# Three edits in the recurrence of a four-layer graph kernel: earlier masks on GpSimd, and a DRAM round trip issued by ScalarE

## The chip, the cores and the metric

The kernel runs on one core of one Trainium2 chip. The metric is the device time of one execution in microseconds, lower being better. Engines are named as in the profile: PE (TensorE, with PEld for its weight loads), DVE (VectorE), ACT (ScalarE), POOL (GpSimd) and SP (SyncE, which here only issues DMAs and waits).

## The reference

Four layers over x and adj, both of shape 64 x 256 x 256 in float32; each layer is followed by a residual and a layer norm. Only layer 0 is touched. It is a gated recurrence over the 256 nodes of each of the 64 graphs:

```python
d = jnp.sum(adj, axis=-1)
dinv = jnp.where(d != 0, 1.0 / jnp.where(d != 0, d, 1.0), 0.0)
norm_adjT = jnp.swapaxes(adj, 1, 2) * dinv[:, :, None]

def step(h, i):
    x = jnp.take(h_e, i, axis=1)
    row = jnp.take(norm_adjT, i, axis=1)
    x_par = jnp.einsum('bj,bjd->bd', row, h)
    iou = x @ W_ioux.T + b_ioux + x_par @ W_iouh.T + b_iouh
    r, z = jnp.split(iou, 2, axis=1)
    r, z = (jax.nn.sigmoid(r), jax.nn.sigmoid(z))
    hc = jnp.tanh(x @ W_coux.T + b_coux + x_par * r @ W_couh.T + b_couh)
    h_new = z * x_par + (1.0 - z) * hc
    h = jax.lax.dynamic_update_slice(h, h_new[:, None, :], (0, i, 0))
    return (h, None)
h_out, _ = jax.lax.scan(step, h_e, jnp.arange(n))
```

h starts as x itself, so the parent sum x_par of node i takes the new states of nodes j < i and the inputs x of nodes j >= i, weighted by adj[j, i] / d[i]. Layers 1 to 3 (a graph convolution and two attentions) follow graph by graph.

## The kernel before

The step over the nodes is serial, and all 64 graphs go through it together: a tile holds 128 partitions, two halves of the 256 features times 64 graphs. One step is a chain: the parent sum xp is transposed on PE (L610), copied by ACT (xpT, L612), multiplied with the weights on PE (L603), put through a sigmoid by ACT (L826), multiplied by xp on DVE (L828), transposed and copied again (rT), multiplied, put through tanh by ACT (L860), and combined on DVE to the next xp (L862, L865). The xp of the next step also takes v (DVE L851), which needs `ready` (POOL L802), the sum gathered so far for that node.

The sums of a block of U = 8 nodes lie in a tile ACC. They are gathered from several sides:

- The x side (nodes j >= i, whose state is still x). For the first 128 nodes it is done ahead of the recurrence. For the others `x_side` does it in 16 groups of 4 graphs beside steps 0 to 79: a tile xA (adj, 128 x 4 x 128) and a tile xX (x) are loaded on SP, xA is multiplied by the triangle `tri` on POOL (`cut`, L332), matmuls follow on PE (L212), and the product goes to DRAM (Us). `x_side` is a generator that the steps with p = n mod 8 of 4 to 7 advance, when no matmul of the early side is at hand.
- The early side: whole earlier blocks of states, read back from DRAM (Hs, with A from adj), multiplied on PE (L416) and sent through DRAM (Es).
- The late side (`late`): states of the last blocks, kept in a ring Hw in SBUF, against a table An, which is adj's tile `raw` masked by a window on POOL (`late_load`, L477). There is one table for each 32 nodes. Its matmuls (PE L519) run in steps p = 0 to 3; ACT copies the products to lb (L255); `send` writes lb to DRAM as Lb in two DMAs (L499), `receive` reads it back as late_sb one step later (L505), and POOL adds it to ACC after the steps p = 5 and 6 (L874).
- The nearest states, added on DVE (L628) and POOL (L661, L665).

The order on each engine is written out by hand: the instructions stand on each engine in the order in which the Python emits them, and each engine works through its own in order. `at_step(n, f)` emits f at the end of step n, after the step's own instructions. Loads of the x side, the early side and the tables go through a list sorted by rank (`load_later`), of which two are issued in each step with p < 4 (`next_load`); `landed` is a guess that is true from three steps after the issue. `cut` of `late_load` first issues what is left of its four loads. All these DMAs are on SP's queue, and so are sends, receives and the DMAs that put each new state hs into the ring (L654). In the built program a DMA takes one of eight completion semaphores, and before it is issued its engine waits until the DMA that used that semaphore last has landed.

Of the kernel before, what the change touches and what calls it, by code (L numbers as in the profile page):

```python
# [70 lines left out]
def _recurrence(tc, ident, Hd, x, adj, W_ioux, b_ioux, W_iouh, b_iouh, W_coux, b_coux, W_couh, b_couh, wide, then):  # L71
# [19 lines left out]
    nc = tc.nc  # L91
    B, N, D = x.shape
# [6 lines left out]
    XB = 4  # L99
    NG = B // 4  # L100
    HB = B // 2
    FAR = (2, 4, 4, 4, 4, 4, 3, 4)

    with ExitStack() as ctx:
# [84 lines left out]
        for w in range(2):  # L189
            first = (w * T - W + T // 2) % W  # L190
# [18 lines left out]
        def x_product(pb, at, A, Xs):  # L209

            for jc, (a, xs) in enumerate(zip(A, Xs)):
                nc.tensor.matmul(  # L212
                    pb[:, at, :], a, xs, start=(jc == 0), stop=(jc == len(A) - 1)
                )

        def x_out(half, b, ub):

            for c in range(2):
                nc.sync.dma_start(
                    Us[c, b:b + 4, half * P:(half + 1) * P, :].rearrange("b i f -> i b f"),  # L220
                    ub[:, :, c * P:(c + 1) * P],
                )
# [26 lines left out]
        def next_load(n):  # L249
            if loads:  # L250
                loads.pop(0)[1](n)

        def copy_later(out, in_, then=None):
            def f(n):
                nc.scalar.copy(out, in_)  # L255
                held.pop(0)
                if then:
                    then(n)

            copies.append(f)  # L260

        def load_later(out, in_, rank):

            begun = []

            def f(n):
                with nc.allow_non_contiguous_dma(reason="bias vector across partitions"):
                    nc.sync.dma_start(out, in_)
                begun.append(n)

            loads.append((rank, f))
            loads.sort(key=lambda e: e[0])
            return begun

        def landed(begun, n):

            return all(f and n > f[0] + 2 for f in begun)

        def at_step(n, f):
            transfers.setdefault(n, []).append(f)  # L280
# [3 lines left out]
        def base_bank(shape, name):  # L284

            while len(held) == 3:
                next_of(copies, now)
            held.append(name)
            return ps.tile(shape, F32, tag="base", name=name, bufs=3)
# [29 lines left out]
        ahead = []  # L319

        def x_side():

            def load(g):
                A = stream.tile([P, XB, P], F32, tag="xA", name=f"xA2_{g}", bufs=3)
                Xs = stream.tile([P, XB, D], F32, tag="xX", name=f"xX2_{g}", bufs=3)
                return A, Xs, [
                    load_later(to, of.rearrange("b j d -> j b d"), 2)
                    for to, of in ((A, adj[g:g + XB, P:N, P:N]), (Xs, x[g:g + XB, P:N, :]))
                ]

            def cut(A):
                nc.gpsimd.tensor_mul(A, A, tri.unsqueeze(1).to_broadcast([P, XB, P]))  # L332

            tiles = [load(e * XB) for e in range(3)]
            ahead = False
            n = yield
            for g in range(0, B, XB):
                A, Xs, last = tiles.pop(0)
                while not ahead:
                    if landed(last, n):  # L340
                        cut(A)
                        ahead = True
                    n = yield
                ub = stream.tile([P, 4, D], F32, tag="ub", name=f"xu2_{g}")
                for b in range(0, XB, 2):
                    pb = base_bank([P, 2, D], f"xp2_{g}_{b}")
                    for q in range(2):
                        x_product(pb, q, [A[:, b + q, :]], [Xs[:, b + q, :]])
                        if q:
                            copy_later(ub[:, b:b + 2, :], pb, None if b + 2 < XB else (  # L350
                                lambda n, b=g, ub=ub: at_step(n + 1, lambda: x_out(1, b, ub))
                            ))
                            if b + 2 == XB:
                                ahead = bool(tiles) and landed(tiles[0][2], n)
                                if ahead:
                                    cut(tiles[0][0])
                                if g + 3 * XB < B:
                                    tiles.append(load(g + 3 * XB))
                        n = yield


# [90 lines left out]
        def late_load(k, n=None):  # L452


            An = blk.tile([P, HB, U, T // U], F32, tag="An", name=f"An_{k}")
            raw = stream.tile([P, HB, T], F32, tag="raw", name=f"raw_{k}", bufs=1)
            first, last = k * T - W + T // 2, k * T + T // 2
            if first < 0:
                nc.gpsimd.memset(raw, 0.0)
            begun = []  # L460
            for lo, hi, at in ring(max(first, 0), last):
                for g in range(2):
                    to = raw[g * W + at:g * W + at + hi - lo]
                    of = adj[g * HB:(g + 1) * HB, lo:hi, k * T:(k + 1) * T].rearrange(
                        "b j i -> j b i"
                    )
                    if n is None:
                        nc.scalar.dma_start(to, of)
                    else:
                        begun.append(load_later(to, of, 1.5))  # L470

            def cut(lo):
                while not all(begun):
                    next_load(now)
                part = raw[:, lo:lo + HB // 4].rearrange("p b (s u) -> p b s u", u=U)
                take = window[k % 2].rearrange("p (s u) -> p s u", u=U).unsqueeze(1)
                nc.gpsimd.tensor_mul(  # L477
                    An[:, lo:lo + HB // 4].rearrange("p b u s -> p b s u"), part,
                    take.to_broadcast(list(part.shape)),
                )  # L480

            for e in range(4):
                if n is None:
                    cut(e * HB // 4)
                else:
                    at_step(n + 20 + e, lambda e=e: cut(e * HB // 4))
            return An

        def late(first):

            k, i = divmod(first, T)
            An = tables[k]["An"]
            lb = stream.tile([P, NG, D], F32, tag="lb", name=f"lb_{first}", bufs=1)
            Lb = dram.tile([2, NG, 4, U, P], F32, tag="Lb", name=f"Lb_{first}")
            sides[first] = blk.tile([P, U, P], F32, tag="late", name=f"late_sb_{first}", bufs=1)

            def send():
                for c in range(2):
                    nc.sync.dma_start(  # L499
                        Lb[c].rearrange("n q u f -> (q u) n f"),  # L500
                        lb[i // U::T // U, :, c * P:(c + 1) * P],
                    )

            def receive():
                nc.sync.dma_start(sides[first], Lb.rearrange("c n q u f -> (c n q) u f"))  # L505

            def then(n):
                at_step(n, send)
                at_step(n + 1, receive)

            n = yield
            for u in range(0, NG // 2, 2):
                pb = [base_bank([P, 2, D], f"late_{first}_{u}_{g}") for g in range(2)]
                for e in range(2):
                    for q in range(4):
                        for g in range(2):
                            rows = slice(g * W, (g + 1) * W)
                            b = (u + e) * 4 + q
                            nc.tensor.matmul(  # L519
                                pb[g][q * T:(q + 1) * T, e, :],  # L520
                                An[rows, b].rearrange("p u s -> p (u s)"),
                                Hw[rows, b, :], start=True, stop=True,
                            )
                    if e:
                        for g in range(2):
                            at = g * NG // 2 + u
                            copy_later(
                                lb[:, at:at + 2, :], pb[g],
                                then if g and u + 2 == NG // 2 else None,
                            )  # L530
                    n = yield
# [137 lines left out]
        sides = {}  # L669
# [8 lines left out]
        with tc.tile_pool(name="r_first_ps", bufs=4, space=bass.MemoryType.PSUM) as xps:  # L678
            for g in range(0, B, GB):
# [4 lines left out]
                for n in range(0, GB, 4):  # L684
                    ub = fst.tile([P, 4, D], F32, tag="ub", name=f"xu_{g}_{n}")
                    for e in range(0, 4, 2):
                        pb = xps.tile([P, 2, D], F32, tag="x", name=f"xp_{g}_{n}_{e}")
                        for q in range(2):
                            b = n + e + q
# [66 lines left out]
        for now in range(N):  # L756
            n = now
# [30 lines left out]
            r, c = rc[:, 0, :], rc[:, 1, :]  # L788
# [685 lines left out]
```

## Time and profile before

| | |
|---|---|
| Median of 3 runs | 3467.49 us (3466.55 to 3467.74) |
| The profiled execution's own time | 3469.95 us |
| Its span, first to last instruction | 3468.2 us |
| Mean granted TensorE clock | 0.976 |
| Recurrence, read from the trace | about 139 to 1560 us |
| Layers 1 to 3 | about 1560 to 3468 us |

How to read it: busy time is counted for each engine, without the instructions that only wait or issue DMAs. A line of the waits reads "engine tile line <- what ended the wait: us in total, times, longest". A line of the timeline reads start, duration, engine, source line, operation, tile written <- tiles read, and in brackets the idle time of the engine just before it with what ended it. A q after an engine's name is its queue of DMA issues.

### The profile page before, as it was taken

What the parts mean: (1) busy time and instruction counts of PE and PEld (TensorE: products, weight loads), DVE (VectorE), ACT (ScalarE), POOL (GpSimd) and SP (SyncE); (2) the same over time, 40 slices, a digit from 0 to 9 for tenths busy, and PEclk for the clock granted to TensorE, in tenths of its full rate; (3) what the DMA queues carried; (4) which work ended last, traced back from release to release, by engine and by line L of the source; (5) the groups of instructions that cost most, each with busy time, mean ns of one, the idle gap of its engine ahead of it and who ended that gap; (6) DMA issues with size and microseconds to landing.
All of it is one profiled execution on the core that took longest, in us unless ns stands there. A gap on an engine that the chain in (4) does not pass through costs nothing.

```text
span 3468.2 us, 80349 instructions
## 1 busy us (share of the span) xinstructions
PE 3243.9 (94%) x29350; PEld 2331.3 (67%) x29350; DVE 2505.5 (72%) x7061; ACT 1883.5 (54%) x5010; POOL 1874.3 (54%) x2165
## 2 busy tenths in 40 slices
PE   5699999899899898887999999999999999999997
PEld 4555555555555555555888888888888888888885
DVE  3376766766666777754888888887888887888885
ACT  0254545545444454444666666666666666666664
POOL 2366676766566777743444444444444444444443
PEclk8999999999999999997999999999999999999999
DMA  9755576687787575321111111111111111111100
GB/s 293 228 156 138 159 178 153 154 187 194 188 207 166 143 174 146 97 58 58 47 46 47 47 47 46 47 47 46 47 46 46 47 47 46 47 47 46 47 29 21
DMA packets 389348, 347.89 MB, mean 100 GB/s; under 512 B 107356, under 2 KB 355304, under 8 KB 383720
## 3 DMA queue, kind: packets, MB, share of 16 engines
q1 hardware_dynamic: 371256, 325.82, 35.0%
q10 hardware_dynamic: 17696, 16.91, 1.5%
q8 instruction: 235, 3.85, 0.5%
q14 instruction: 161, 1.32, 0.1%
HBM read 224.01 MB, written 99.61 MB: 93 GB/s over the span
## 4 chain that ended last, share of the span: by engine, by line
PE 73%; DVE 7%; DMA 7%; POOL 5%; issue 4%; ACT 3%; SPq 2%; ACTq 0%; DVEq 0%; POOLq 0%
PE mm L995 13%; PE rc L603 5%; PE s L1179 4%; PE rc L595 4%; PE mm_2f L995 3%; PE mm_3v L995 3%; PE mm_t L995 3%; PE late L519 3%; PE mm_3f L995 3%; PE mm_2v L995 3%; PE mm_g L995 3%; PE mm_2s L995 3%; DVE ACC L628 3%; PE o L1214 3%; PE mm_2w L995 3%
## 5 line engine op out<-in xcount | busy, mean ns | idle before, releaser
L628 DVE SCALAR_TENSOR_TENSOR ACC<-keep,S,ACC 128x128 f32<-128x128 f32 x1712 | 504.3, 345 | 189.9 <-ACT hs L646 172.4
L1191 POOL TENSOR_TENSOR p3s<-p 128x256 f32<-128x256 f32 x512 | 387.6, 788 | 366.5 <-ACT p L1189 366.0
L995 PE MATMUL mm<-xT,weights 128*128 128x256 f32 x2048 | 481.9, 383 | 2.9 <-ACT xT L1077 2.9
L995 PEld LDWEIGHTS mm<-xT,weights 128*128 128x128 f32 x2048 | 384.8, 190 | 79.4 <-issue 25.5
L1188 DVE TENSOR_TENSOR p<-s,neg 128x512 f32<-128x512 f32 x512 | 317.7, 683 | 114.3 <-PE s L1179 114.3
L665 POOL TENSOR_TENSOR ACC<-ACC,far 128x384 f32<-128x384 f32 (+1 forms) x313 | 372.6, 1190 | 24.5
L595 PE MATMUL rc<-WxT,xqT 128*64 128x256 f32 x2048 | 330.2, 401 | 4.2 <-ACT rc L836 1.2
L661 POOL TENSOR_TENSOR far<-hs,S 128x384 f32<-128x384 f32 (+1 forms) x313 | 304.9, 974 | 4.7
L802 POOL TENSOR_TENSOR ready<-ACC,dinv 128x128 f32<-128x128 f32 x255 | 102.3, 401 | 369.6 <-DVE ACC L628 369.4
L959 ACT ACTIVATE y<-y,shift,rstd 128x256 f32<-128x256 f32 x512 | 273.4, 599 | 48.0 <-DVE shift L957 43.8
L1189 ACT ACTIVATE p<-p 128x512 f32<-128x512 f32 x512 | 295.0, 627 | 2.1 <-DVE p L1188 1.6
L1102 ACT ACTIVATE qk<-mm,weights 128x256 f32<-128x256 f32 x256 | 107.5, 471 | 268.9 <-PE mm L995 268.9
L1091 POOL TENSOR_TENSOR y<-y,g 128x512 f32<-128x512 f32 x64 | 81.1, 1267 | 267.5 <-issue 267.5
L1228 DVE RECIPROCAL rT<-o 128x256 f32<-128x256 f32 x128 | 223.8, 1748 | 0.3 <-PE o L1205 0.2
L947 DVE BATCH_NORM_STATS2 st<-y 128x6 f32<-128x256 f32 x512 | 209.0, 408 | 13.4 <-POOL y L1091 12.7
L951 POOL TENSOR_TENSOR rstd<-rstd,mhalf 128x2 f32<-128x2 f32 x256 | 173.8, 697 | 82.5 <-DVE rstd L950 80.7
L612 ACT COPY xpT<-xpT_ps 128x128 f32<-128x128 f32 x256 | 68.4, 267 | 259.7 <-PE xpT_ps L610 259.7
L603 PE MATMUL rc<-WhT,xpT 128*64 128x128 f32 x2048 | 171.3, 289 | 29.1 <-ACT xpT L612 28.6
L1056 POOL TENSOR_TENSOR dis<-dis,mhalf 128x2 f32<-128x2 f32 x64 | 44.9, 702 | 277.3 <-DVE dis L1055 260.7
L603 PEld LDWEIGHTS rc<-WhT,xpT 128*64 128x64 f32 x2048 | 108.4, 138 | 119.9 <-ACT xpT L612 84.2
L212 PE MATMUL xp<-xX,xA 128*128 128x256 f32 x384 | 115.7, 446 | 59.3 <-POOL xA L681 32.6
L1154 ACT ACTIVATE qk<-mm,weights 128x256 f32<-128x256 f32 x256 | 107.5, 471 | 115.9 <-PE mm L995 115.9
(162 smaller groups left out, 7501.7 us busy)
## 6 DMA issues: line engine op xcount, KB each, us to landing
xX<-in_x_dram ACTq DMA_DIRECT2D x16, 1024.0 KB
Us<-xu SPq DMA_DIRECT2D x64, 256.0 KB
xq<-in_x_dram SPq DMA_DIRECT2D x64, 256.0 KB
ACC<-Us SPq DMA_DIRECT2D x32, 512.0 KB
Es<-eu SPq DMA_DIRECT2D x64, 256.0 KB
early_sb<-Es SPq DMA_DIRECT2D x32, 512.0 KB
xin<-in_x_dram SPq DMA_DIRECT2D x64, 256.0 KB
ad<-in_adj_dram SPq DMA_DIRECT2D x64, 256.0 KB
```

The source lines that it names most:

```text
L595: nc.tensor.matmul(G[o * B:(o + 1) * B], xqT[a, i // 2][:, i % 2, kc, h * B:(h + 1) * B], WxT[:, kc, o, gates], start=False, stop=False, s ...
L603: nc.tensor.matmul(G[o * B:(o + 1) * B], hT[:, kc * B:(kc + 1) * B], WhT[:, kc, o, g], start=False, stop=(kc == 1), skip_group_check=True,)
L628: nc.vector.scalar_tensor_tensor(acc[:, 0, :], keep[:, j % 2, :], s, acc[:, 0, :], ALU.mult, ALU.add)
L661: nc.gpsimd.tensor_mul(tmp[:, 0:count, :], hs.unsqueeze(1).to_broadcast(shape), s.unsqueeze(2).to_broadcast(shape),)
L665: nc.gpsimd.tensor_add(acc, acc, tmp[:, 0:count, :])
L947: nc.vector.bn_stats(st, y[:, c, :])
L959: nc.scalar.activation(y[:, c, :], y[:, c, :], AF.Identity, bias=shift[:, c:c + 1], scale=rstd[:, c:c + 1],)
L995: nc.tensor.matmul(pm[:, c, :], lhsT[:, k, c * P:(c + 1) * P], rhs[:, k, :], start=(k == 0), stop=(k == 1),)
L1188: nc.vector.tensor_add(p, s_ps[i], self.neg3)
L1189: nc.scalar.activation(p, p, AF.Exp, scale=ISQ)
L1191: nc.gpsimd.tensor_add(both, p[:, 0, :], p[:, 1, :])
L1228: nc.vector.reciprocal(rT, o_ps[:, 1, :])
```

## The change

Three edits, all in layer 0:

1. `x_side` looks for the next group's tile at each of its turns and masks it as soon as its loads count as landed, instead of only at the last matmul of the group before it.
2. The four masks of a late table are emitted at the ends of steps 12, 15, 20 and 23 of the 32 before the table is needed, instead of 20, 21, 22, 23.
3. `send` and `receive` of the late side are issued by ACT instead of SP.

```diff
@@ x_side
                     n = yield
+                ahead = False
                 ub = stream.tile([P, 4, D], F32, tag="ub", name=f"xu2_{g}")
...
-                            if b + 2 == XB:
-                                ahead = bool(tiles) and landed(tiles[0][2], n)
-                                if ahead:
-                                    cut(tiles[0][0])
-                                if g + 3 * XB < B:
-                                    tiles.append(load(g + 3 * XB))
+                            if b + 2 == XB and g + 3 * XB < B:
+                                tiles.append(load(g + 3 * XB))
+                        if not ahead and tiles and landed(tiles[0][2], n):
+
+                            cut(tiles[0][0])
+                            ahead = True
                         n = yield
@@ late_load
-                    at_step(n + 20 + e, lambda e=e: cut(e * HB // 4))
+                    at_step(n + (12, 15, 20, 23)[e], lambda e=e: cut(e * HB // 4))
@@ late
             def send():
                 for c in range(2):
-                    nc.sync.dma_start(
+                    nc.scalar.dma_start(
                         Lb[c].rearrange("n q u f -> (q u) n f"),
                         lb[i // U::T // U, :, c * P:(c + 1) * P],
                     )
 
             def receive():
-                nc.sync.dma_start(sides[first], Lb.rearrange("c n q u f -> (c n q) u f"))
+                nc.scalar.dma_start(sides[first], Lb.rearrange("c n q u f -> (c n q) u f"))
```

## The prediction

> **What bounds the kernel now.** I first read the busy time by stages (stretches 0 to 139, 139 to 1560, 1560 to 3468 us). The 256 recurrence steps, layer 0, are the middle one, and all three edits lie in it. The last stage, with PE busy for 1868.80 of 1908.20 us, has none of their instructions.
>
> ```profile
> 0.00:139.00 139.00, 82.16 (x308) 64.00 (x308) 39.63 (x61) 2.83 (x4) 28.35 (x21) 0.82 0.95 286
> 139.00:1560.00 1421.00, 1292.94 (x16498) 766.57 (x16493) 976.55 (x3348) 700.31 (x2445) 964.09 (x1056) 0.98 0.63 156
> 1560.00:3468.20 1908.20, 1868.80 (x12550) 1500.72 (x12550) 1489.34 (x3653) 1180.33 (x2561) 881.91 (x1088) 0.99 0.14 45
> ```
>
> (Busy us of PE, PEld, DVE, ACT, POOL; PE's clock; DMA share; GB/s.) No engine is full here: a step is a chain PE transpose, ACT copy, PE, ACT sigmoid, DVE, PE, ACT tanh, DVE. I took each step's length from the timeline, as the distance between starts of the xpT transposes (PE L610). With p = n mod 8, the medians for p = 0 to 7 are 5.31, 5.16, 5.16, 5.47, 5.51, 5.14, 4.96, 5.46 us, so anything over about 6 is a stall. Their waits over the stretch:
>
> ```profile
> POOL ACC L874 <- DMA late_sb<-Lb: 40.0, 10, 7.5
> DVE keep L851 <- POOL ready L802: 25.3, 9, 5.4
> PEld xp L212 <- POOL xA L332: 16.5, 7, 3.0
> PE xp L212 <- POOL xA L332: 13.7, 7, 2.6
> POOL An L477 <- DMA raw<-in_adj_dram: 8.9, 1, 8.9
> ```
>
> Two kinds are what the edits aim at. **Kind A**: a matmul of the x side stands in PE's order ahead of the chain's own rT transpose, and waits for its mask on POOL. Step 31:
>
> ```profile
> 312.15 1.04 POOL L661 TENSOR_TENSOR far<-hs,S 128x512 f32<-128x512 f32 x1
> 313.27 1.26 POOL L665 TENSOR_TENSOR ACC<-ACC,far 128x512 f32<-128x512 f32 x1
> 314.49 1.26 POOL L332 TENSOR_TENSOR xA<-xA,tri 128x512 f32<-128x512 f32 x1
> 315.81 0.91 PE L212 MATMUL xp<-xX,xA 128*128 128x256 f32 x2 [2.55 <-POOL xA L332]
> ```
>
> **Kind B**: POOL waits for late_sb, `ready` stands behind it, and DVE waits for that. Step 142:
>
> ```profile
> 943.20 1.26 POOL L874 TENSOR_TENSOR ACC<-ACC,late_sb 128x512 f32<-128x512 f32 x1 [7.45 <-DMA late_sb<-Lb]
> 944.42 0.40 POOL L802 TENSOR_TENSOR ready<-ACC,dinv 128x128 f32<-128x128 f32 x1
> 944.85 0.36 DVE L851 SCALAR_TENSOR_TENSOR keep<-keep,Sd,ready 128x128 f32<-128x128 f32 x1 [5.41 <-POOL ready L802]
> ```
>
> late_sb is late because SP is: SP's own waits, and what an issue costs it (ns, least/median/most):
>
> ```profile
> SPq L499 <- ACT lb L255: 143.4, 16, 23.3
> SPq L505 <- DMA Lb<-lb: 15.1, 17, 1.8
> L499 SPq DMA_DIRECT2D Lb<-lb x60: 619/646/7224, 202.9 to 1499.2; - x60
> ```
>
> [...] on ACT the same wait would hold the sigmoids. [...] from 48 to 49 us, with ACT's x loads beside SP's, I count 241 packets on SP's queue and 244 on ACT's. [...] The clock records agree: 0.5 for 3.4 us from 261.6, 316.2, 442.5, 497.1 and 582.4 us, right after kind A, and for 6.8 from 896.4 and 944.2, after kind B.
>
> **Part 1, xA masks.** No instruction is added. In the built order the sixteen masks (1268 ns each) keep their count, and the late ones move: from step 14 to 12 and 13, 22 to 20, 31 to 28, 46 to 45, 54 to 52 and 53, 63 to 60, 78 to 77. Their loads had landed before those steps (for step 28, at 291.1 us in step 27), so POOL should not wait for them. The seven kind A steps (14, 22, 31, 46, 54, 63, 78) took 6.91, 9.17, 9.97, 7.85, 9.24, 9.89, 9.04; over their medians that is 1.95 + 4.2 + 4.5 + 2.9 + 4.3 + 4.4 + 4.1 = 26. POOL has about 1.5 us idle ahead of `ready` in a step (369.4 us over 203 waits is 1.8), which covers the moved 1.27; without it a step pays up to 1.27. Taken: **-26**, bounds -27 to -13.
>
> **Part 2, late table.** Four masks of 736 ns per table, formerly after steps 20 to 23, stand after 12, 15, 20, 23. At 12 the loop that forces outstanding loads comes first. For tables 2, 3, 6, 7 the four raw DMAs landed one step or more earlier (table 7 in step 203, mask after 204): nothing. For tables 4 and 5 the fourth raw load is forced at steps 108 and 140, on SP, behind Hw DMAs and on a completion semaphore that the second Lb send used last, so SP can issue it only after Lb has landed: about 747 and 936 us on the old clock. Raw loads took 5 to 11 us to land, so 753 to 757, and 942 to 946. POOL reaches the mask at 746 and 935, `ready` stands behind it, and v needs `ready` some 3 us later: 5 to 9 us, twice. Before, the fourth load of table 5 held POOL from 980.7 to 984.3, and cost its step 1.0; that goes. Taken: **+13**, bounds 0 (rows that land at once) to +18.
>
> **Part 3, the way through DRAM.** 60 sends and 30 receives leave SP for ACT. ACT around one send and receive now:
>
> ```profile
> 787.34 0.61 ACT L255 COPY lb<-late 128x512 f32<-128x512 f32 x1
> 788.85 0.27 ACT L612 COPY xpT<-xpT_ps 128x128 f32<-128x128 f32 x1 [0.89 <-PE xpT_ps L610]
> 794.13 0.59 ACT L255 COPY xqT<-xqT_ps 128x512 f32<-128x512 f32 x1 [1.50 <-PE xqT_ps L576]
> 794.62 0.27 ACT L612 COPY xpT<-xpT_ps 128x128 f32<-128x128 f32 x1
> ```
>
> Sends: two issues of 0.65 us plus gaps are 1.36, between the last lb copy and the next xpT copy, where ACT is idle for 0.74 to 1.58. What sticks out, summed over 30, is **+9**. ACT's own loads issued in 0.37 to 0.9 mostly, 2.57 once, beside SP issues of 1 to 4, so I take SP's median and not its 7.2; bounds 0 to +30. Receives: they stand between the xqT copy and the xpT copy, which follow without a gap; an issue is 0.34, or nothing if it runs under the copy. Taken **+4**, bounds 0 to +13.
>
> The receive also waits for Lb, now on ACT, 6.0 to 7.0 us after the last lb copy. In 18 of 30 rounds Lb landed 3.3 to 4.1 us after it: no wait. In the 12 others (about 295, 475, 655 to 1040 without 788, 1250, 1375) it took 6.5 to 13.0, part of it SP's delay in issuing, part packets ahead. Without the first but with packets alternating against SP's 4 and 8 KB ones I estimate 5 to 10; the excess over 6.4 adds up to **+14**, most of it at 877 to 1025. Bounds 0, and +42 if Lb lands no earlier than before. Behind this wait are xpT, hs and every later step on PE and DVE.
>
> What goes: kind B in steps 126, 134, 142, 150, 158 (7.61, 8.89, 9.69, 7.58, 8.86 over 4.96), **-18**; the half-clock steps after them (127, 135, 143, 151, 159, together 11 over the median), **-9**, since 151 also has degree work on DVE. late_sb lands some 10.5 after the lb copy, and POOL comes for it at 10.3 to 11.2. SP, freed of the L499 waits, brings Hw sooner: step 112 lost 4.8 to it, **-4**. [...] **+4** for half clocks.
>
> **Sum**: -26 + 13 + 9 + 4 + 14 - 18 - 9 - 4 + 4 = -13. The profiled execution took 3469.95 us (span 3468.2), 2.5 above the median of three, 3467.49; the same steps make both, so 3467.5 - 13 = 3454.5.
>
> **Rivals.** *The wait moves to ACT* (slower): if Lb's packets do no better on ACT's queue than on SP's, the receives cost 42 and not 14, with half clocks some 5 more: -13 + 33 = +20, 3487. It decides from 27 us of receive wait in all. For it: large SP packets at 920 to 930 us (8 KB, about 30 per us). Against: Lb no longer waits until SP comes round, up to 9.1 us after the copy. *Gains are only half kept* (no change): kind A steps end on `ready` or late_sb next, saving 13, and the rest cancels: about 3467. Against: the v instruction of step 31 was done at 313.9, before the mask began. *Costs hidden*: receives and forced loads cost nothing, -13 - 31 = -44, 3424. That nothing moves is excluded for part 1 by the built order.
>
> **Numbers.** Forecast (a gain of over 0.2%, 7 us, which is about what a measurement of this kernel can tell from no change) 0.42, costs hidden 0.10: faster 0.52. Half kept 0.17. Slower 0.31. Range 3428 to 3486.
>
> **What would show it.** Right: no L212 wait on xA L332; steps 14 to 78 near 5; L874's wait for late_sb under 10 us; ACT waiting for Lb ahead of xpT around 880 to 1040; POOL waiting for raw near 750 and 940. Wrong: ACT waits at sends, long ACT issues, or stalls in quiet rounds.

## The result and the profile after

The changed kernel took 3508.53 us (median of 4 runs, 3503.64 to 3514.11) against 3467.02 for the kernel before (4 runs): a ratio of 1.0123, 95% interval 1.0105 to 1.0141. It is slower by 41.5 us where 13 less were forecast. Every source line from L344 on is one higher than before: L499, L505, L654 are now L500, L506, L655, and L416, L519, L802, L851, L874 are L417, L520, L803, L852, L875.

The busy time by stages (columns as before):

```profile
140.00:1601.00 1461.00, 1304.11 (x16496) 775.28 (x16492) 973.37 (x3347) 701.59 (x2445) 962.66 (x1056) 0.96 0.61 152
1601.00:3509.60 1908.60, 1870.04 (x12550) 1501.57 (x12550) 1489.55 (x3654) 1179.51 (x2561) 880.67 (x1088) 0.98 0.14 45
```

The recurrence took 40 us longer (1461.0 for 1421.0), and layers 1 to 3 were unchanged (1908.6 for 1908.2). No engine did more work: DVE, ACT and POOL are within 4 us of before, and PE's 11 us more are for as many matmuls at a mean granted clock of 0.96 instead of 0.98. The loss is waiting. Some of the engines' waits in the recurrence (tile, what ended the wait: us in total, times, longest):

```profile
POOL ACC L875 <- DMA late_sb<-Lb: 29.5, 22, 5.5
PEld early L417 <- issue: 26.5, 80, 7.7
POOL An L478 <- DMA raw<-in_adj_dram: 18.7, 2, 10.0
PE early L417 <- DMA A<-in_adj_dram: 13.2, 3, 7.5
DVE keep L852 <- POOL ready L803: 11.0, 3, 4.8
PEld late L520 <- DMA Hs<-Hd: 7.6, 1, 7.6
PE late L520 <- DMA A<-in_adj_dram: 7.4, 1, 7.4
PE late L520 <- DMA Hw<-hs: 5.9, 1, 5.9
```

What the forecast aimed at is gone or smaller: of L212's waits for xA 0.5 us is left, DVE waits 11.0 us for `ready` instead of 25.3, and POOL 29.5 for late_sb instead of 40.0 (the forecast's sign of being right was under 10). New are PE's waits at L417, for A and Hs of the early side, and at L520. L520 reads only the ring Hw and An, so the rows that name Hs and A there need a second look: the longest of these stalls, in step 160, ended at 1078.05 us, when a ring DMA (Hw) issued at 1071.96 had landed at 1077.95; an Hs and an A were landing at the same time. So L520's new waits are for the ring. PE and PEld are two views of one stall, so these rows do not add up.

The same view for SP's queue, all its waits for Lb or late_sb:

```profile
SPq L655 <- DMA late_sb<-Lb: 96.8, 23, 6.3
SPq L655 <- DMA Lb<-lb: 62.2, 29, 4.5
SPq L237 <- DMA Lb<-lb: 28.7, 3, 11.1
SPq L315 <- DMA Lb<-lb: 23.7, 4, 8.1
SPq L268 <- DMA late_sb<-Lb: 15.1, 2, 8.0
SPq L268 <- DMA Lb<-lb: 14.3, 5, 13.0
SPq L315 <- DMA late_sb<-Lb: 5.6, 1, 5.6
SPq L300 <- DMA Lb<-lb: 4.2, 1, 4.2
```

These are the lines to stop at. None of these issues has anything to do with Lb: L655 puts hs into the ring, L237 sends dinv, L315 and L268 load ACC, A and Hs, L300 loads rows. Yet SP stood 250.6 us behind Lb's DMAs, which it no longer issues: 133.1 us in 42 waits behind ACT's sends (Lb) and 117.5 in 26 behind its receives (late_sb). Before, its only such waits were those of its own receive, 15.1 us. What ties them is the completion semaphore. The trace has the number of the semaphore with every DMA: in the kernel before, SP's 1111 DMAs of the recurrence take 100, 102, 103 and so on to 108, eight in all, and start over, without an exception; after, ACT's 90 sends and receives take theirs out of the same row, and with SP's 1021 fill it without a gap. In both traces all 1527 DMAs (of 1535) that follow another on the same semaphore went out after that one's last landing signal. In every one of the 68 waits the semaphore waited for is the one that SP's next DMA itself takes, and the one that used it last was ACT's.

Another line of the view is new:

```profile
SPq L655 <- PE late L520: 130.8, 15, 21.2
```

SP no longer stands at L499 until ACT has copied the late products to lb (143.4 us before). Most of that time it now stands at L655, in nearly the same rounds, until PE's late matmuls, whose products those are, have run.

One place in full: SP's and ACT's issues and the early side in steps 92 and 93 of the changed kernel, from the timeline:

```profile
645.96 1.29 ACTq L500 DMA_DIRECT2D Lb<-lb  x2
648.51 0.46 SPq L237 DMA_DIRECT2D dinv<-deg  x1
649.30 0.34 SPq L315 DMA_DIRECT2D ACC<-Us  x1
649.69 0.43 SPq L268 DMA_DIRECT2D Hs<-Hd  x1
652.58 0.33 ACTq L506 DMA_DIRECT2D late_sb<-Lb  x1
657.29 0.33 SPq L268 DMA_DIRECT2D A<-in_adj_dram  x1
657.41 1.26 POOL L875 TENSOR_TENSOR ACC<-ACC,late_sb 128x512 f32<-128x512 f32 x1 [0.77 <-DMA late_sb<-Lb]
...
660.03 1.08 PE L417 MATMUL early<-Hs,A 80*32 80x256 f32 x8 [7.51 <-DMA A<-in_adj_dram]
```

A's load stands right behind Hs in SP's order, but goes out 7.6 us after it, at 657.29, just when late_sb has landed (POOL goes on at 657.41): it takes semaphore 103, as ACT's receive at 652.58 had done. PE's matmul of the early side, ahead of the rT transpose in PE's order, waited 7.51 us, and step 93 took 15.74 us instead of 5.14. In the kernel before, A was issued in step 91, one microsecond after ACC:

```profile
648.26 0.53 SPq L315 DMA_DIRECT2D ACC<-Us  x1
648.89 0.37 SPq L268 DMA_DIRECT2D Hs<-Hd  x1
649.31 0.42 SPq L268 DMA_DIRECT2D A<-in_adj_dram  x1
```

In units of steps, the first A of the early blocks for nodes 64, 96 and 128 went out at 26.9, 59.0 and 91.1 before, and at 28.5, 60.5 and 93.3 after. PE's order takes them in steps 29, 61 and 93 in both.

### The profile page after: what moved, and what is told of

The parts are those of the page before. It is cut to its first block, busy times and chain, and to the rows that moved or that the text cites. A ratio compares the mean times of both kernels' runs of the same rounds, so it can differ in the third digit from the quotient of the medians.

```text
span 3509.6 us, 80234 instructions
## 1 busy us (share of the span) xinstructions
PE 3254.0 (93%) x29350; PEld 2339.6 (67%) x29350; DVE 2500.6 (71%) x7061; ACT 1883.9 (54%) x5010; POOL 1871.3 (53%) x2165
## 4 chain that ended last, share of the span: by engine, by line
PE 74%; DMA 8%; DVE 6%; ACT 3%; POOL 3%; issue 3%; SPq 1%; ACTq 1%; DVEq 0%; POOLq 0%
PE mm L996 13%; PE rc L604 5%; PE rc L596 4%; PE s L1180 4%; PE mm_2f L996 3%; PE mm_3v L996 3%; PE mm_t L996 3%; PE late L520 3%; PE mm_3f L996 3%; PE mm_2v L996 3%; PE mm_g L996 3%; PE mm_2s L996 3%; PE mm_2w L996 3%; PE o L1215 3%; DVE ACC L629 3%
## 5 line engine op out<-in xcount | busy, mean ns | idle before, releaser
L803 POOL TENSOR_TENSOR ready<-ACC,dinv 128x128 f32<-128x128 f32 x255 | 101.9, 399 | 410.8 <-DVE ACC L629 410.6
L1103 ACT ACTIVATE qk<-mm,weights 128x256 f32<-128x256 f32 x256 | 107.3, 470 | 269.0 <-PE mm L996 269.0
L1057 POOL TENSOR_TENSOR dis<-dis,mhalf 128x2 f32<-128x2 f32 x64 | 44.8, 700 | 277.3 <-DVE dis L1056 260.8
L520 PE MATMUL late<-Hw,An 64*32 64x256 f32 x3840 | 156.7, 391 | 23.5 <-issue 10.2
L863 DVE TENSOR_TENSOR zcc<-zc,rc 128x128 f32<-128x128 f32 x256 | 72.6, 284 | 146.2 <-ACT rc L861 144.4
```

The costliest lines, as they stand in the source:

```text
L520: nc.tensor.matmul(pb[g][q * T:(q + 1) * T, e, :], An[rows, b].rearrange("p u s -> p (u s)"), Hw[rows, b, :], start=True, stop=True,)
```

## The experiments

Theories. **T1**: the shared completion semaphores tie SP's queue to ACT's order (part 3), and SP's loads come late. **T2**: the four loads that part 2 forces push the early side's loads back (part 2). **T3**: ACT's own waiting and issuing, or Lb's packets on a second queue, cost the time (part 3, but not by semaphores). The ratios are to the kernel before on the same chip, whose medians were 3464.3 to 3466.3 us; 1% is 34.7 us.

**Parts apart.** The edits are those of the diff, alone or left out.

Part 1 alone: 

> Part 1 of the change alone (xA's masks taken up as soon as the tile should be there). All theories: the seven kind A steps lose their 23 us, as in the changed kernel, and nothing else moves: about 3444 us (3438 to 3450). A time above 3460 would say that the earlier masks themselves cause part of the loss elsewhere.

Measured 3443.97 us, 0.9938 (0.9924 to 0.9952). The seven steps of kind A fall by 1.3 to 4.4 us, 23.0 in all, as in the changed kernel.

Part 2 alone: 

> Part 2 alone (late table's masks after steps 12, 15, 20, 23). T1 (Lb's DMAs on ACT's queue hold SP's issue through the shared completion semaphores): only the waits for raw at steps 109 and 141 with their half clocks, some +10, and SP's loads of the early side stay in time: 3472 to 3482. T2 (the forced loads push the early side's loads back on SP, and that is the main loss): +40 or more, 3507 and up, with PE waiting for A at L417 in steps 29, 61, 93, 157.

Measured 3457.68 us, 0.9981 (0.9972 to 0.9990): faster by 8 us, so T2 falls, and so does the forecast's sign for this part. The stalls for raw came as expected (steps 109, 110 and 141 longer by 4.0, 2.6 and 7.1).

Part 3 alone: 

> Part 3 alone (sends and receive of Lb on ACT). T1 and T3 (ACT's own waiting and issuing): +45 to +60 with kind A's stalls still there, 3510 to 3525; under T1 PE waits for late loads (A, Hs, Hw) make up more than half of it and SP's waits behind Lb are 100 us or more, under T3 the lost time is at ACT's receives and sends (under 40 us in all) and the loads come in time. T2 (part 2 is the cause): part 3 gains by kind B, below 3467.

Measured 3530.31 us, 1.0191 (1.0173 to 1.0210): the whole loss is here. SP's waits behind Lb are those of the full change:

```profile
SPq L654 <- DMA late_sb<-Lb: 99.4, 24, 6.4
SPq L654 <- DMA Lb<-lb: 62.8, 31, 4.4
```

Steps 29, 61, 93, 128, 154, 157, 160, 223 and 224 are longer by 4.0, 6.3, 9.3, 8.8, 5.3, 5.5, 10.5, 5.3 and 5.7: 60 us in nine steps.

Parts 1 and 2: 

> Parts 1 and 2 with the sends and the receive left on SP (part 3 undone). T1 and T3: the early side's loads are in time again, -23 from part 1 and +10 from part 2, 3450 to 3460. T2: still slower than before, 3490 or more.

Measured 3441.92 us, 0.9933 (0.9914 to 0.9952), better than expected. It is only 2 us below part 1 alone, less than the two intervals can tell apart: beside part 1, that part 2 gains anything is not shown. Against it the full change, 3508.53, puts part 3 at +66.6.

**Is it the semaphores?** Ninety tiny loads, with Lb left on SP:

```diff
@@ send (in the loop, ahead of each DMA) and receive
+                    tiny(c)
...
+                tiny(2)
@@
+        spare = const.tile([16, 3, 4], F32, name="spare")
+        def tiny(e):
+            nc.scalar.dma_start(spare[:, e, :], x[0, 0:16, 0:4])
```

On ACT: 

> The kernel before, Lb's sends and receive left on SP, and 90 added loads of 256 bytes (16 x 4 floats of x into a tile that nobody reads) issued by ACT at the places in its order where the changed kernel has its sends (two) and its receive (one). They wait for no Lb. T1 (the completion semaphores, taken in turn by the DMAs of both queues, tie SP's issue to ACT's order): SP waits for these loads, 50 us or more in all, and PE for late A, Hs or Hw: +15 to +60, 3480 to 3525. T3 (what costs is ACT's wait for Lb and Lb's packets on a second queue): only ACT's issue time, as the change had it at p = 4, +5 to +12, 3471 to 3478.

Measured 3565.35 us, 1.0284 (1.0260 to 1.0307): 99 us lost though all of Lb's transfers stayed on SP, above what T1 expected. The timeline of steps 26 to 29:

```profile
295.23 0.41 SPq L268 DMA_DIRECT2D xA<-in_adj_dram  x1
301.26 0.32 ACTq L672 DMA_DIRECT2D spare<-in_x_dram  x1
301.62 0.43 ACTq L672 DMA_DIRECT2D spare<-in_x_dram  x1
302.71 0.40 SPq L268 DMA_DIRECT2D xX<-in_x_dram  x1
303.26 0.39 SPq L315 DMA_DIRECT2D ACC<-Us  x1
308.21 0.32 ACTq L672 DMA_DIRECT2D spare<-in_x_dram  x1
309.69 0.33 SPq L268 DMA_DIRECT2D Hs<-Hd  x1
310.06 0.42 SPq L268 DMA_DIRECT2D A<-in_adj_dram  x1
```

SP stands for 7.1 us until ACT, in its own order, has issued the first tiny load and it has landed, and for 6.0 us again for the third. A goes out in step 29, and steps 29, 61, 62, 93 and 190, stalls of the changed kernel, are longer by 8.4, 5.5, 3.4, 7.5 and 7.0. A further 38 us lie in steps 126, 158, 176, 208 and 222, where the changed kernel has no such loss: there SP's own receive or ring DMAs went out late after waits for tiny loads (in step 126 POOL waited 13.95 us for late_sb). In all, SP waits 187 us for tiny loads that nobody reads, 43.0 of them here:

```profile
SPq L268 <- DMA spare<-in_x_dram: 43.0, 6, 10.4
```

The same loads on SP (`nc.sync` in `tiny`): 

> Control: the same 90 small loads at the same places of the program, issued by SP. T1 and T3: [...] no queue waits for another's order: -2 to +10, 3464 to 3476, and under T1 clearly below the kernel with the loads on ACT.

Measured 3495.78 us, 1.0084 (1.0062 to 1.0106). The control is dearer than expected: its 90 issues took SP 69 us (median 0.58 each, against 0.32 on ACT). Which of them cost the kernel its 29 us was not followed up. But it is 70 us below the kernel with the loads on ACT, and steps 29, 61 and 93 are as before.

**Which of ACT's DMAs?** Only `send`, then only `receive`, on `nc.scalar`.

Sends: 

> Only the sends on ACT, the receive left on SP (which waits there for Lb in SP's order, as before). T1: SP may run on past the sends, but stands at the receive until Lb has landed, and its semaphores hang on ACT's sends, which ACT issues early in its order: half of part 3's loss or less, +5 to +30. T3 by ACT's issue time: +9 for the issues, and no more.

Measured 3507.92 us, 1.0131 (1.0103 to 1.0159). Receive: 

> Only the receive on ACT, the sends left on SP. T1: the receive is the DMA that ACT reaches late (some 7 us after the last lb copy), so SP's waits behind it and the late loads of A, Hs and Hw are here: +30 to +60, 3497 to 3527. T3 by ACT's wait for Lb: late sends make Lb land late and ACT wait, +20 to +45, with the time in ACT's wait ahead of xpT and the loads in time.

Measured 3507.79 us, 1.0115 (1.0089 to 1.0141). Either half costs some 40 us, and both together 66. With the sends on ACT, SP still stands behind them (135.7 us for Lb in all, 44.8 of it its own receive), and steps 29, 61 and 93 stall; the loss is above T1's range of 5 to 30. With the receive on ACT, the same steps stall (3.7, 6.1 and 2.0 us longer), and T3 has its share too:

```profile
SPq L654 <- DMA late_sb<-Lb: 130.6, 28, 6.1
ACT xpT L612 <- DMA Lb<-lb: 30.4, 8, 7.9
```

The sends come late in SP's order, so Lb lands late, and now the sigmoids' engine waits for it. The steps with p = 5 are 68 us longer in all.

**A queue that shares no semaphore with SP.** Parts 1 and 2, and both of Lb's DMAs on `nc.gpsimd`: 

> Parts 1 and 2, and Lb's sends and receive on POOL's own queue, which neither SP nor ACT shares. T1: if POOL's DMAs have completion semaphores of their own, SP waits for no Lb and late_sb, PE's waits for late A, Hs and Hw are gone, kind B and kind A are gone too, and what is lost stands at POOL (its issues and its wait for Lb, with `ready` behind it, at 30 rounds of 1 to 5 us): 3430 to 3560, the size of POOL's loss being open. T3 (traffic on a second queue delays SP's loads): loads late as in the changed kernel, PE waiting at L417 and L520 for A, Hs and Hw.

Measured 3471.24 us, 1.0022 (1.0014 to 1.0030): 29 us above parts 1 and 2 alone, and 37 below the full change. SP never waits for Lb or late_sb: in the trace POOL's 90 DMAs take eight semaphores of their own (111 to 118). Steps 29, 61, 93, 157, 160, 190, 223 and 224 are within 2.3 us of their lengths with parts 1 and 2; two steps are longer, 136 by 6.6, where PE waits for the ring Hw, and 154 by 6.0, where PE stands 4.0 us between two matmuls of L520 and the profile names no wait. Much of the rest stands at POOL:

```profile
SPq L655 <- ACT hs L647: 181.3, 72, 6.2
...
POOL late_sb L506 <- DMA Lb<-lb: 27.2, 12, 5.1
DVE keep L852 <- POOL ready L803: 54.0, 42, 4.8
```

The first line is SP's queue, which now waits longest for the states hs that it is to send; the others are the engines. With parts 1 and 2 alone DVE's wait for `ready` is 33.3 us in 10 places. Lb's packets run on a second queue here too (31.5 MB on it in the recurrence), so the traffic half of T3 falls. The issuing engine is another as well, so this run alone does not clear ACT's own waits; the tiny loads do, for which ACT waits for no Lb.

**Can PE wait it out?** The full change, with the early side taking its loads a step later:

```diff
-                if not early_in or not landed(early_in[0][0], n):
+                if not early_in or not landed(early_in[0][0], n - 1):
```

> The whole change, and the early side takes a load as landed one step later (four steps after its issue in the program and not three), so that PE's order comes to it about 5 us later. T1 (SP late by the semaphores; PE waits at L417 in steps 29, 61, 62, 93, 127, 157, 190 for some 36 us in the changed kernel): most of these waits shrink by up to 5 us each, 15 to 30 less, 3479 to 3494. T3 (ACT's own waiting and issuing): no such gain, 3503 to 3515. Against both: the early side's products fill PE in other steps then.

Measured 3523.63 us, 1.0188 (1.0163 to 1.0213): a miss. Steps 29, 61, 93 and 190 lost their stalls (3.6, 5.7, 10.5 and 3.0 us), but the time came back in the steps behind them: 32, 63, 64, 70, 71, 79 and 96 are longer by 4.8, 3.2, 3.9, 3.6, 3.0, 3.9 and 8.6. In 32, 64 and 96 PE waits at L520, which needs the ring (3.2, 1.9 and 6.4 us). The wait moved; that the queue behind it is still late fits with this, and SP still stood 267 us behind Lb's DMAs.

**Parts 1 and 2 without the stall.** The loads of a table forced after n + 12 as in part 2, the masks later:

```diff
+            if n is not None:
+                at_step(n + 12, force)
...
-                    at_step(n + 20 + e, lambda e=e: cut(e * HB // 4))
+                    at_step(n + (15, 18, 20, 23)[e], lambda e=e: cut(e * HB // 4))
```

`force` is the loop that stood at the head of `cut`. 

> Parts 1 and 2 with Lb on SP, and the table's four loads forced after step n+12 as in part 2, but the four masks after 15, 18, 20, 23, so that POOL comes to the first three steps after the force. Theory: the waits for raw at steps 109 and 141 (with the half clocks after them some 13 to 15 us in the kernel with parts 1 and 2) go, the early force keeps its gains at 112, 144 to 151, 163, 183, 215: 3427 to 3436. Rival: the forced loads push Lb's DMAs and Hw back just the same, and what POOL no longer waits for raw it waits for late_sb: 3438 to 3445, no better than parts 1 and 2.

Measured 3434.79 us, 0.9923 (0.9905 to 0.9941), the fastest of all, 29 us below before and 74 below the change. POOL no longer waits for raw, and steps 109 and 141 are back at 5.14. But 112 and 142 to 144, which parts 1 and 2 had at 5.30, 7.19, 4.96 and 5.30, are 7.50, 8.79, 7.42 and 6.22. This suggests that part of the gain at 112 and 144 was only the stall just before, in which the late DMAs caught up. The run's interval overlaps that of parts 1 and 2; that it is the better of the two is likely, not shown.

## Why the prediction was wrong

It gave 3454.5 with a range of 3428 to 3486; the median lies 22.5 us beyond the upper end. The main error is one term of part 3, off by 70 us; the error in part 2 took 19 us off it, which was luck.

- **Part 1, -26: right.** The seven steps lost 1.3, 3.6, 4.4, 2.3, 3.7, 4.3 and 3.1, together 22.7; alone it brought 22 us. No rival of half the gain: `ready` did not stand next.
- **Part 2, +13: wrong in sign.** The stalls for raw were sized right (13.7 us alone, 109, 110 and 141). What was left out, it seems, is that the next waits, for Hw and late_sb, were then partly served: 112, 142, 143 and 144 fell by 4.8, 2.2, 2.0 and 0.8. Steps 150, 151, 163, 183 and 215 fell by 12.9 more in all; why is open. Step 126 took 2.7 more. That makes -6; the medians differ by 8, and smaller differences in other steps are not accounted for.
- **Part 3, sends +9: right.** The p = 4 steps are 7.4 us longer than in the kernel with parts 1 and 2, and 9.5 longer than before; each issue took ACT 0.64 us in the median, 1.57 at most.
- **Receive's issue +4: too high.** It took 0.33 us, and in 23 of the 30 rounds ran wholly under the xqT copy.
- **Receive's wait +14, half clocks +4: right.** Steps 101, 109, 117, 133, 141 and 149 are 17.0 us longer than with parts 1 and 2; in them ACT's receive goes out only when Lb has landed. The rival that gave 42 here did not happen. Two readings of this term need care. That packets of the two queues alternate was the author's estimate: the forecast's count, 241 and 244 in one microsecond, shows equal shares and no more. And what brings a half clock on was not shown: those of the recurrence before lasted 3.4 us or multiples of it, but ahead of the five that the forecast ties to kind A, PE had been idle for only 1.7 to 2.6 us at a stretch, and for 3.9 and 4.7 us ahead of the two that it ties to kind B.
- **Kind B -18 and the half-clock steps -9: right.** The ten steps that it named fell by 23 us against parts 1 and 2 and by 25 against the kernel before. The eight that fell against parts 1 and 2 (110, 126, 134, 135, 150, 151, 158 and 159) fell by 24.
- **The step that failed: "SP, freed of the L499 waits, brings Hw sooner", -4.** SP was not freed. It exchanged 213 us of its own waits at L499 and L505 for 130.8 us behind the late matmuls and 250.6 us behind ACT's DMAs, and no longer ran ahead: in the recurrence it waited 694 us in all, where it had waited 532. The 130.8 are not the loss, since the kernel with Lb on POOL has 147.9 of them and its loads in time. Step 112 gained nothing from part 3 (+0.3 with it alone, though with only the sends or only the receive on ACT it fell by 3.0 and 4.8); in the changed kernel that gain was part 2's. The new stalls (steps 29, 61, 62, which follows one at half clock, 93, 128, 154, 157, 160, 190, 223 and 224), measured against the kernel with parts 1 and 2, are 3.7 + 5.8 + 2.4 + 10.6 + 7.4 + 5.4 + 5.8 + 9.9 + 4.5 + 5.5 + 5.0 = **66 us** where the sum had -4.

With 7 + 17 - 24 + 66 = 66, part 3 is accounted for (the two profiled spans differ by 65.4, of which 62.4 in the steps; the steps not named come to -4): what was forecast of it cancels, and what was not forecast is its whole cost. That the stalls at 29, 61, 93 and 157 are the semaphores' is seen in the issue times, which meet the landings of ACT's DMAs. At 190 and 223 SP had stood 13.0 us (until 1229.3) and 11.1 and 5.6 us (until 1404.5 and 1411.8) behind Lb's DMAs, shortly ahead of the issues that came late. For 128, 160 and 224 it rests on SP's queue being later throughout, and on these stalls being gone with Lb on POOL (128 is 1.4 us longer there than with parts 1 and 2, the other two are not). Step 154 is as long there, and the profile names no wait for its 3.5 us pause of PE, so the cause of its 5.4 is open.

The fact needed was in the description of the kernel: eight semaphores, and an engine waits for a semaphore's last user (in the traces, 1527 times out of 1527). The forecast even used it for raw in part 2, within one queue. It was not asked what it means once two queues take from the same eight. The move did not even save SP the time of its issues, because it paid more in waits (250.6 us) than it had paid for these 90 issues (65 us).

Two of the three signs listed for an error, waits at sends and long issues on ACT, stayed away, because the loss was on the queue that had been relieved. The third came: stalls in quiet rounds, on PE at steps 190 and 224, and at 223 on ACT, whose copy to hs waited 3.57 us for a ring DMA.

## What to carry to other kernels

When a DMA moves to another engine's queue, write down which completion semaphore it takes and who takes it next. Here both queues drew in turn from one row of eight: in the changed kernel 264 of SP's 1021 DMAs in the recurrence went out ahead of one that ACT had yet to issue, by one to seven places of the common order in 263 cases and by nine in one. Nor did the moved transfer have to be large: loads of 256 bytes on ACT held SP for 187 us. Look in the queue's waits for lines that name a tile the waiting DMA neither reads nor writes; that can be such a tie. Make sure of it by the semaphore, since the profile can also name the wrong one of several waits, as it did at L520. And count a stall as lost only after the next step that had been waiting anyway.

## What was not expected of the hardware

- Small loads were not cheap on SP's queue: 90 loads of 256 bytes took SP 0.58 us each to issue in the median, 7.4 at most, 69 us in all, and the kernel took 29 us longer. On ACT the median was 0.32 us.
- DMAs issued by GpSimd took that engine 0.69 us (sends) and 0.60 us (receives) each in the mean, and tied nothing to SP's queue: SP had no wait for Lb or late_sb, and the 90 DMAs took eight semaphores of their own (111 to 118).
- The issue of a DMA on ACT ran under the copy before it: in 23 of the 30 rounds the receive's 0.33 us lay wholly inside the xqT copy (in step 93 it ran from 652.58 to 652.91, the copy until 653.02).
